# Graph attention on one core: the first three turned A^T pairs move into the set-up's last block

## The chip, the core and the metric

The kernel runs on 1 core of one Trainium2 chip. A core has five engines that run at the same time, each with its own queue of instructions: TensorE (PE, matrix products; its weight loads are shown as PEld), VectorE (DVE), ScalarE (ACT), GpSimd (POOL) and SyncE (SP). In this kernel POOL and SP mostly issue transfers (DMA) between the device's memory and the on-chip memory. An instruction waits until the work that it needs, on another engine or of a transfer, has been done; behind it the whole queue of its engine waits. [...]

The metric is the device time of one execution, in microseconds (us). The time before is 2067.35 us, the median of 3 runs (2067.16 to 2067.58).

## The reference

Two layers on N = 4096 nodes with 512 features; the change is in the first, a graph attention with H = 8 heads of 64 features. Cut to what matters:

```python
feats = jnp.einsum('nf,hfo->hno', X, W)
s_self = jnp.einsum('hno,ho->hn', feats, a_self)
s_neigh = jnp.einsum('hno,ho->hn', feats, a_neigh)
dense = s_self[:, :, None] + s_neigh[:, None, :]
dense = jnp.where(dense > 0, dense, ALPHA * dense)
dense = dense * A[None, :, :]
attn = jax.nn.softmax(dense, axis=-1)
out = jnp.einsum('hij,hjo->hio', attn, feats) + b[:, None, :]
out = jnp.transpose(out, (1, 0, 2)).reshape(N, H * FH)
return jax.nn.relu(out)
```

The result is added to x and normalized by row. The second layer (an attention inside groups of 128 nodes) follows; the change does not touch it. A, the 4096x4096 adjacency, holds zeros and ones.

## The kernel before

The exponential of a score is a product of a factor of the row and a factor of the column, and the choice between the two slopes is a maximum. So the kernel never forms a softmax over N x N scores: for a tile of 128 neighbours j and a chunk of 1024 nodes it computes Q = max(p, d_j) * A^T on VectorE (L1386), and a mark (which of the two was larger, L1391 and L1395), and lets TensorE sum Q, A^T and the marks against tables of the features.

**Set-up** (the block of pools at L586 and after) makes these tables. It works in 8 blocks k of 4 tiles of 128 nodes:

- turn_rows transposes the rows of x (L650), and ScalarE copies them out (L653).
- features (L722) multiplies a tile with the weights; VectorE adds the bias (L733). exponentials turns the two scores of a tile into its factors: two products on VectorE (L664), then three exponentials on ScalarE (e_all L670, pu_j L671, d_all L672).
- scaled_features makes the two tables of a tile: one scaled on VectorE (L766), one split into two float32r parts, by ScalarE (L775) and VectorE (L776). Each two tiles POOL writes them to memory (g_d and f_d, L789).
- rows_of_exponentials turns the factors of a block into rows (L695 on TensorE, the copy pu_row on ScalarE L699, the write pu_d on POOL L703). columns_of_exponentials turns these rows back into columns in another order (L708) and VectorE copies them to pu_all (L709).
- In the last block also the column sums of the features are made: the sums of x times the weights (L561), a copy to S_part on ScalarE (L820), and after all features four small products to columns (L568) and S_col on VectorE (L827).
- parts_of_exponentials splits factors into parts on VectorE (nb_all L676, e_b and rest L683 to L690).
- Three loads of adjacency, a_b, four tiles each in 8-bit floats, are issued by POOL in between (L581, after blocks 1, 3 and 5).

**Pass 0** follows. A pass handles two heads; there are four, each over 4 chunks c of 1024 nodes. Inside a chunk the 32 tiles j are taken in groups of 8 (in pass 0). For a group TensorE does, in this order: the products of A^T (accf, L1406: 32 matmuls), the products of Q (acc, L1426: 128), the sums of the marks (dens, L1440: 32) and counts (ae, L1350: 16).

In pass 0, A^T does not exist yet: `bring` makes it. For a pair of tiles TensorE turns a_b by 8 transposes of 128x128, two 8-bit values seen as one bf16 (L1130), into a PSUM bank given by `misc`, and ScalarE casts the bank to the two tiles `at` (L1134), which POOL also writes to at_d for the later passes (L1135). The first group's four pairs are brought right before its Q, and then in each group two pairs of the next group before the Q products and two after the counts:

```python
if at_step == 0:
    for j in cycle:
        bring(0, 0, j)
```

`misc` takes the PSUM banks of a list in turn. The list holds one bank in set-up, and from pass 0 on a second, that of the pool opened with the accumulator ae. `at` comes from 6 buffers of the pool atp, and from a second pool with 6 more, which lies where set-up's tiles were; `ring` counts turns to choose between them. Q has 6 + 2 buffers in the same manner.

**What sets the order.** TensorE's instructions stand in the order in which the program issues them (manual_schedule). For the other engines a scheduler orders instructions by its own estimates, with every dependency kept; keep_in_program_order pins single ones. A tile that lies over memory of a closed pool waits for all who used that memory, transfers too: the first `at` of the second pool waits for set-up's last writes.

Of the kernel before, what the change touches and what calls it, by code (L numbers as in the profile page):

```python
# [19 lines left out]
P = 128  # L20
# [375 lines left out]
F32R = mybir.dt.float32r  # L396
# [8 lines left out]
def adjacency_streamed_path(  # L405
# [29 lines left out]
    nc = tc.nc  # L435
# [6 lines left out]
    BIG = 2.0**70  # L442
    MORE = 6
    FP8 = mybir.dt.float8e4
    C = 1024
    CT = C // P
# [4 lines left out]
    scale = 1.0 / float(F) ** 0.5  # L451
# [13 lines left out]
    at_d = dram.tile([NCH, NT, P, C], F32, name="at_d")  # L465
# [21 lines left out]
    ident_b = const.tile([P, P], BF16, name="ident_b")  # L487
# [3 lines left out]
    d_all = const.tile([P, NT, H], F32, name="d_all")  # L491
# [3 lines left out]
    nb_all = const.tile([P, NT, H], F32, name="nb_all")  # L495
# [75 lines left out]

    ats = {}
    a_bs = {}
    pools = {}
    pools["adj"] = first_pass.enter_context(tc.tile_pool(name="adjp", bufs=3, side="right"))

    def load_adjacency(c, j):

        a_b = pools["adj"].tile([P, CT, 4 * P], FP8, name="a_b8")
        a_bs[c, j] = a_b  # L580
        return nc.gpsimd.dma_start(  # L581
            a_b, adj[ts(c, C), j * P : (j + 4) * P].rearrange("(t p) n -> p t n", p=P)
        )


    with tc.tile_pool(name="setup1", bufs=1, side="right") as one, tc.tile_pool(  # L586
        name="setup2", bufs=2, side="right"
# [69 lines left out]
        def exponentials(k, u, sc):  # L657

            j = 4 * k + u
            if u == 0:  # L660
                pu_js[k] = two.tile([P, 4, 2, H], F32, name="pu_j")
            st = small.tile([P, 5, H], F32, name="st")
            for lo, hi, w in ((0, 3, 1), (3, 5, 0)):
                nc.vector.tensor_tensor(  # L664
                    st[:, lo:hi].rearrange("p k (q h) -> p k q h", q=2),
                    sc[:, None, :, :, w].to_broadcast([P, hi - lo, 2, H // 2]),
                    powers[:, lo:hi].rearrange("p k (q h) -> p k q h", q=2),
                    OP.mult,
                )
            nc.scalar.activation(e_all[:, j], st[:, 0:2], AF.Exp)  # L670
            nc.scalar.activation(pu_js[k][:, u], st[:, 3:5], AF.Exp)  # L671
            nc.scalar.activation(d_all[:, j, :], st[:, 2], AF.Exp)  # L672
# [19 lines left out]
        def rows_of_exponentials(k):  # L692
            pr = pss.tile([2 * H, 4, P], F32, name="ps_set")
            for u in range(4):
                nc.tensor.transpose(  # L695
                    pr[:, u, :], pu_js[k][:, u].rearrange("p k h -> p (k h)"), ident
                )
            row = rows[k] = late.tile([2 * H, 4 * P], F32, name="pu_row")
            nc.scalar.copy(  # L699
                row.rearrange("p (q n k) -> p q k n", q=2, k=2),  # L700
                pr.rearrange("p (q k) n -> p q k n", q=2),
            )
            nc.gpsimd.dma_start(pu_d[:, ts(k, 4 * P)], row)  # L703

        def columns_of_exponentials(k):
            pc = pss.tile([P, 4, 2 * H], F32, name="ps_set")
            for u in range(4):
                nc.tensor.transpose(pc[:, u, :], rows[k][:, ts(u, P)], ident[: 2 * H, : 2 * H])  # L708
# [83 lines left out]
        for k in range(NB):  # L792
            for u in range(4):
                features(k, u)
                if u == (0 if k else 2) and k + 1 < NB:
                    turn_rows(k + 1)
                    if k + 2 < NB:
                        load_rows(k + 2)
                if u == 1 and k:
                    rows_of_exponentials(k - 1)  # L800
                if u == 2 and k:
                    columns_of_exponentials(k - 1)
                if u == 2 and k == 0:
# [309 lines left out]

    checked = []

    def bring(r, c, j):

        if r:
            at = ats[r, c, j] = ring("at", atp, 6).tile([P, C], F32R, name="at")
            nc.sync.dma_start(at.bitcast(F32), at_d[c, j])  # L1120
            return
        if j % 2:
            return
        if j % 4 == 0 and (c, j) not in a_bs:
            load_adjacency(c, j)
        pairs = a_bs[c, j - j % 4].rearrange("p t n -> p (t n)").bitcast(BF16)
        pairs = pairs.rearrange("p (t k n) -> p t k n", t=CT, k=2)[:, :, j % 4 // 2, :]
        pt = misc([P, CT, P], BF16)
        for t in range(CT):
            nc.tensor.transpose(pt[:, t, :], pairs[:, t, :], ident_b)  # L1130
        both = pt.rearrange("p t n -> p (t n)").bitcast(FP8).rearrange("p (n k) -> p n k", k=2)
        for k in range(2):
            at = ats[r, c, j + k] = ring("at", atp, 6).tile([P, C], F32R, name="at")
            nc.scalar.copy(at, both[:, :, k])  # L1134
            nc.gpsimd.dma_start(at_d[c, j + k], at.bitcast(F32))  # L1135

    def load_block():

        k = len(checked)
# [185 lines left out]
    def main_pass(r, ae=None, wide=4):  # L1325

        for c in range(NCH):
# [33 lines left out]
            for j0 in range(0, NT, wide):  # L1361
# [19 lines left out]
                for j in cycle:  # L1381
                    for h in range(2):
                        hh = 2 * r + h
                        q = qs[j, h] = ring("q", qp, 6).tile([P, C], F32, name="q")
                        d_j = d_all[:, j, hh : hh + 1]
                        nc.vector.scalar_tensor_tensor(  # L1386
                            q, p_row[h], d_j, ats[r, c, j].bitcast(F32), op0=OP.max, op1=OP.mult
                        )
                        mark = marks[j, h] = sgp.tile([P, C], FP8, name="mark")
                        if j % 4 == 3 and h == 1:  # L1390
                            nc.vector.tensor_scalar(  # L1391
                                mark, q, d_j, None, op0=OP.is_gt, saturate=False
                            )
                        else:
                            nc.scalar.activation(  # L1395
                                mark,
                                q,
                                AF.Sigmoid,
                                bias=nb_all[:, j, hh : hh + 1],
                                scale=BIG,  # L1400
                                saturate=False,
                            )
                for j in cycle:
                    for w in range(2):
                        for s in range(2):
# [142 lines left out]
```

## Time and profile before

| | before |
|---|---|
| median of 3 runs | 2067.35 us (2067.16 to 2067.58) |
| the profiled execution's own time | 2069.35 us |
| its span, from first to last instruction | 2067.6 us |
| TensorE busy | 2032.2 us (98%) |
| VectorE busy | 1670.1 us (81%) |
| ScalarE busy | 1540.2 us (74%) |
| mean granted TensorE clock | 0.993 |
| accf, 2048 matmuls | 494.4 us, 398 ns each |
| acc, 8192 matmuls | 902.8 us, 593 ns each |
| casts of A^T on ScalarE | 128, 120.1 us, 1025 ns each |
| end of the last features of set-up | 156.28 us |
| start of the first accf | 164.90 us |

All times in the profile are us from the start of the span unless marked ns. The chain that ended last is followed back from the last instruction: at each step to what released it, or to the instruction before it on its engine. "Issue" is time in which an engine waited for nothing that the profile shows. In rows of the timeline the bracket at the end tells how long the engine had been idle and what ended that. The granted clock is that of TensorE, as a share of full speed.

### The profile page before, as it was taken

The numbers are of one execution on the slowest core, as the hardware profiler recorded it, in microseconds if no ns is written. First come the engines' busy times: TensorE is split into PE (matmuls) and PEld (weight loads), VectorE is DVE, ScalarE is ACT, GpSimd is POOL, SyncE is SP. The second block draws the span as 40 slices with busy tenths as digits, with TensorE's granted clock in tenths as the row PEclk, the third lists the DMA queues.
The fourth block names the chain that finished last, engine by engine and source line by source line (L and its number), as shares of the span: only waits on it lengthen the run. The fifth ranks groups of instructions, "written<-read, shape, count | busy, mean of one in ns | idle before, by whom it ended". The sixth has DMA issues, their size and how long they took to land.

```text
span 2067.6 us, 38274 instructions
## 1 busy us (share of the span) xinstructions
PE 2032.2 (98%) x15086; PEld 1047.3 (51%) x15086; DVE 1670.1 (81%) x2125; ACT 1540.2 (74%) x1869; POOL 222.0 (11%) x361
## 2 busy tenths in 40 slices
PE   8999999999999999999999999999999999999997
PEld 6885555544445444444445444444454444445453
DVE  5667888888799998798999999999975984886654
ACT  3338888888878899788899899998885666567420
POOL 1223222222100000000000000000200210210111
PEclk9999999999999999999999999999999999999998
DMA  6989999999899999888999899989974773774211
GB/s 198 302 272 245 273 291 263 297 257 299 257 344 336 365 344 349 263 312 292 326 311 341 288 364 330 329 285 367 321 240 141 245 254 128 229 275 160 80 49 43
DMA packets 207371, 551.31 MB, mean 267 GB/s; under 512 B 24780, under 2 KB 65740, under 8 KB 207180
## 3 DMA queue, kind: packets, MB, share of 16 engines
q1 hardware_dynamic: 136716, 418.45, 57.8%
q0 software_dynamic: 62272, 121.91, 23.1%
q10 hardware_dynamic: 8192, 8.39, 1.2%
q8 instruction: 121, 1.98, 0.4%
q14 instruction: 70, 0.57, 0.1%
HBM read 491.79 MB, written 107.22 MB: 290 GB/s over the span
## 4 chain that ended last, share of the span: by engine, by line
PE 84%; DMA 6%; DVE 4%; issue 3%; ACT 2%; POOL 1%; ACTq 0%; POOLq 0%; DVEq 0%
PE acc L1426 36%; PE accf L1406 21%; PE ps_m L1067 5%; PE ps_fe L722 5%; PE ps_m L995 5%; PE dens L1440 5%; DMA at_d<-at 3%; DVE q L1386 3%; DMA a_b<-in_adj_dram 2%; PE ps_m L1022 1%; PE ps_m L1081 1%; PE ps_m L1130 1%; DMA xt_f<-in_x_dram 1%; PE ps_m L975 1%; PE ps_m L924 1%
## 5 line engine op out<-in xcount | busy, mean ns | idle before, releaser
L1386 DVE SCALAR_TENSOR_TENSOR q<-p_row,d_all,at 128x1024 f32<-128x1024 f32 x1024 | 1242.4, 1278 | 163.9 <-PE acc L1426 126.5
L1395 ACT ACTIVATE mark<-q,nb_all 128x1024 fp8e4<-128x1024 f32 x896 | 994.3, 1145 | 167.7 <-DVE q L1386 152.6
L1426 PE MATMUL acc<-q,g_s 128*32 128x512 f32 x8192 | 902.8, 593 | 1.1 <-DVE q L1386 0.4
L1426 PEld LDWEIGHTS acc<-q,g_s 128*32 128x32 f32 x8192 | 264.7, 110 | 593.8 <-issue 532.2
L1406 PE MATMUL accf<-at,f_s 128*128 128x512 f32 x2048 | 494.4, 398 | 1.9 <-issue 1.8
L1406 PEld LDWEIGHTS accf<-at,f_s 128*128 128x128 f32 x2048 | 380.2, 189 | 110.7 <-issue 29.1
L1151 ACT ACTIVATE ck<-ck,neg_half_f 128x1024 f32<-128x1024 f32 x128 | 145.9, 1140 | 27.1 <-DMA ck<-in_adj_dram 27.1
L1152 ACT ACTIVATE ck<-ck,neg_quarter 128x1024 f32<-128x1024 f32 x128 | 146.3, 1143 | 1.8
L1440 PE MATMUL dens<-mark,e_b 128*6 128x512 fp8e4 x2048 | 124.5, 379 | 1.6 <-ACT mark L1395 1.6
L722 PE MATMUL ps_fe<-w_sb_f,xT_f 128*128 128x264 f32 (+1 forms) x512 | 121.2, 395 | 4.5 <-ACT xT_f L653 4.5
L1134 ACT CAST at<-ps_m 128x1024 fp32r<-128x1024 fp8e4 x128 | 120.1, 1025 | 5.9 <-ACT mark L1395 3.1
L1067 PE MATMUL ps_m<-wvT,x1T 128*128 128x512 f32 x256 | 114.2, 594 | 0.0
L995 PE MATMUL ps_m<-x1T,M_sb 128*128 128x512 f32 x256 | 113.0, 595 | 0.9 <-ACT x1T L976 0.9
L722 PEld LDWEIGHTS ps_fe<-w_sb_f,xT_f 128*128 128x128 f32 x512 | 100.8, 200 | 18.8 <-ACT xT_f L653 4.9
L1271 POOL DMA_DIRECT2D hs_d<-hst x12 | 10.7, 893 | 832.3 <-DVE hst L1261 814.0
L1391 DVE TENSOR_SCALAR mark<-q,d_all 128x1024 fp8e4<-128x1024 f32 x128 | 95.8, 749 | 4.8
L1440 PEld LDWEIGHTS <-e_b 128*6 128x6 bf16 x2048 | 52.8, 86 | 81.8 <-issue 38.7
L1135 POOL DMA_DIRECT2D at_d<-at x128 | 69.0, 539 | 175.4 <-ACT at L1134 110.0
L995 PEld LDWEIGHTS ps_m<-x1T,M_sb 128*128 128x128 f32 x256 | 48.1, 190 | 62.5 <-issue 60.3
L1067 PEld LDWEIGHTS ps_m<-wvT,x1T 128*128 128x128 f32 x256 | 47.7, 190 | 57.1 <-issue 55.9
L1002 ACT ACTIVATE zT<-ps_m,zb 128x512 f32<-128x512 f32 x32 | 21.8, 682 | 71.1 <-PE ps_m L995 71.1
L1075 DVE TENSOR_TENSOR v_t<-ps_m,bv_row 128x512 f32<-128x512 f32 x32 | 21.9, 685 | 61.5 <-PE ps_m L1067 61.5
(185 smaller groups left out, 1084.2 us busy)
## 6 DMA issues: line engine op xcount, KB each, us to landing
at<-at_d SPq DMA_DIRECT2D x384, 512.0 KB, 6.1
f_s<-f_d SPq DMA_DIRECT2D x128, 512.0 KB, 7.4
at_d<-at POOLq DMA_DIRECT2D x128, 512.0 KB, 14.9
ck<-in_adj_dram SPq DMA_DIRECT2D x128, 512.0 KB, 5.4
g_s<-g_d SPq DMA_DIRECT2D x128, 256.0 KB, 5.9
f_d<-fst POOLq DMA_DIRECT2D x16, 1024.0 KB, 7.2
a_b<-in_adj_dram POOLq DMA_DIRECT2D x32, 512.0 KB, 16.1
p_row<-pu_d SPq DMA_DIRECT2D x32, 512.0 KB, 7.5
```

What stands on the lines that cost most here:

```text
L722: nc.tensor.matmul(pf[:, q, :, cols], tile_j(xTs[k][:, c].rearrange("p u n -> p (u n)"), u), w_sb[:, c, 4 * q : 4 * q + 4, cols], start=(c ...
L995: nc.tensor.matmul(pz, L1["M"][:, f, ts(c, P)], x1T[:, f, :], start=(f == 0), stop=(f == FC - 1),)
L1067: nc.tensor.matmul(pv, x1T[:, f, ts(u, P)], L1["wvT"][:, f, :], start=(f == 0), stop=(f == FC - 1),)
L1134: nc.scalar.copy(at, both[:, :, k])
L1151: tc.keep_in_program_order(nc.scalar.activation(ck, ck, AF.Square, bias=neg_half))
L1152: nc.scalar.activation(ck, ck, AF.Abs, bias=neg_quarter, accum_out=binp[:, k : k + 1])
L1386: nc.vector.scalar_tensor_tensor(q, p_row[h], d_j, ats[r, c, j].bitcast(F32), op0=OP.max, op1=OP.mult)
L1391: nc.vector.tensor_scalar(mark, q, d_j, None, op0=OP.is_gt, saturate=False)
L1395: nc.scalar.activation(mark, q, AF.Sigmoid, bias=nb_all[:, j, hh : hh + 1], scale=BIG, saturate=False,)
L1406: nc.tensor.matmul(accf[:, s, :], f_s[j // 4][:, j % 4, w, :], ats[r, c, j][:, ts(s, HB)], start=(j == 0 and w == 0), stop=(j == NT - 1 an ...
L1426: nc.tensor.matmul(acc[o : o + 32, s, :], g_s[j // 4][:, j % 4, h, o % FH : o % FH + 32], qs[j, h][:, ts(s, HB)], start=(j == 0), stop=(j ...
L1440: nc.tensor.matmul(dens[lo : lo + 6, :], e_b[:, j, 2 * r + h, :], marks[j, h][:, ts(s, HB)], start=(j == 0), stop=(j == NT - 1),)
```

## The change

`bring` moves ahead of set-up, and the first three of the four pairs of the first group are brought inside the last block of set-up: pair 1 after the second tile's features, pair 2 after the third's, pair 3 after the fourth's. Only the fourth pair is brought at the start of pass 0. The columns of the column sums come before rows_of_exponentials of the last block instead of after it. The first group's Q and marks are issued behind set-up's last scores on VectorE and last casts on ScalarE, by a hint to the scheduler (issue_after). `ring` counts turns from the beginning, so that the tiles of set-up count too.

In the scheduled program, the instructions of every engine are as many as before. On ScalarE the casts of the three pairs stand between set-up's last exponentials and copies, the copy of pu_row for the last block stands behind the last of them, and the marks of the first group, 14, follow the casts of the fourth pair in one row (before, the casts of the next pairs stood between them). On VectorE the first Q stands ahead of the last copy to pu_all. On POOL the writes of the three pairs stand between set-up's last writes: g_d and f_d of the last two tiles, then the two writes of pair 3, then pu_d of the last block.

```diff
     def ring(name, pool, n):
 
+        k = turns[name]
+        turns[name] += 1
         if name not in more:
             return pool
-        k = turns[name] % (n + more[name][1])
-        turns[name] += 1
-        return pool if k < n else more[name][0]
+        return pool if k % (n + more[name][1]) < n else more[name][0]
...
+    ends_of_setup = {}
...
+    def bring(r, c, j):
...
+        pt = misc([P, CT, P], BF16)
+        for t in range(CT):
+            nc.tensor.transpose(pt[:, t, :], pairs[:, t, :], ident_b)
+        both = pt.rearrange("p t n -> p (t n)").bitcast(FP8).rearrange("p (n k) -> p n k", k=2)
+        for k in range(2):
+            at = ats[r, c, j + k] = ring("at", atp, 6).tile([P, C], F32R, name="at")
+            ends_of_setup["ACT"] = nc.scalar.copy(at, both[:, :, k])
+            nc.gpsimd.dma_start(at_d[c, j + k], at.bitcast(F32))
...
-                nc.vector.tensor_tensor(
+                ends_of_setup["DVE"] = nc.vector.tensor_tensor(
                     st[:, lo:hi].rearrange("p k (q h) -> p k q h", q=2),
...
+                if k == NB - 1 and u:
+                    bring(0, 0, 2 * u - 2)
                 if k == NB - 1 and u == 1:
                     pS = pss.tile([P, H * FH], F32, name="ps_set")
...
-        rows_of_exponentials(NB - 1)
         pS = pss.tile([P, PR], F32, name="ps_set")
         sums_to_columns(pS, S_part)
         nc.vector.scalar_tensor_tensor(
             S_col, b_col, float(N), pS, op0=OP.mult, op1=OP.add
         )
+        rows_of_exponentials(NB - 1)
         columns_of_exponentials(NB - 1)
...
-    def bring(r, c, j):
...
                 if at_step == 0:
-                    for j in cycle:
-                        bring(0, 0, j)
+                    bring(0, 0, 6)
...
+                with ExitStack() as behind:
+                    if at_step == 0:
+                        for ins in ends_of_setup.values():
+                            behind.enter_context(tc.issue_after(ins.ins))
+                    for j in cycle:
...
```

The body of `bring` is the same but for the line that keeps the last cast; the loop over `cycle` that computes Q and marks is only indented.

More of the change, by code (lines that the diff above doesn't have):

```diff
@@ L583, in load_adjacency @@
         )
+    def bring(r, c, j):
+        if r:
+            at = ats[r, c, j] = ring("at", atp, 6).tile([P, C], F32R, name="at")
+            nc.sync.dma_start(at.bitcast(F32), at_d[c, j])
+            return
+        if j % 2:
+            return
+        if j % 4 == 0 and (c, j) not in a_bs:
+            load_adjacency(c, j)
+        pairs = a_bs[c, j - j % 4].rearrange("p t n -> p (t n)").bitcast(BF16)
+        pairs = pairs.rearrange("p (t k n) -> p t k n", t=CT, k=2)[:, :, j % 4 // 2, :]
+        pt = misc([P, CT, P], BF16)
[6 more added lines that the diff above has]
+            nc.gpsimd.dma_start(at_d[c, j + k], at.bitcast(F32))
     with tc.tile_pool(name="setup1", bufs=1, side="right") as one, tc.tile_pool(
@@ L1114, in adjacency_streamed_path @@
     checked = []
-    def bring(r, c, j):
[L1118 to L1135, printed above, removed]
     def load_block():
@@ L1380, in main_pass @@
                 qs = {}
[L1381 to L1392, printed above, removed]
-                            )
[L1394 to L1402, printed above, removed]
+                with ExitStack() as behind:
[3 more added lines that the diff above has]
+                    for j in cycle:
+                        for h in range(2):
+                            hh = 2 * r + h
+                            q = qs[j, h] = ring("q", qp, 6).tile([P, C], F32, name="q")
+                            d_j = d_all[:, j, hh : hh + 1]
+                            nc.vector.scalar_tensor_tensor(
+                                q, p_row[h], d_j, ats[r, c, j].bitcast(F32), op0=OP.max, op1=OP.mult
+                            )
+                            mark = marks[j, h] = sgp.tile([P, C], FP8, name="mark")
+                            if j % 4 == 3 and h == 1:
+                                nc.vector.tensor_scalar(
+                                    mark, q, d_j, None, op0=OP.is_gt, saturate=False
+                                )
+                            else:
+                                nc.scalar.activation(
+                                    mark,
+                                    q,
+                                    AF.Sigmoid,
+                                    bias=nb_all[:, j, hh : hh + 1],
+                                    scale=BIG,
+                                    saturate=False,
+                                )
```

## The prediction, on record before the changed kernel was run

> **What bounds the kernel now.** The page comes first: TensorE is busy for 98% of the span, and the chain that ended last lies mostly on it. Nothing that leaves TensorE's stream as long as it was can gain, and only a stretch in which TensorE waits, or runs slowly, has something to give.
>
> ```profile
> PE 2032.2 (98%) x15086; PEld 1047.3 (51%) x15086; DVE 1670.1 (81%) x2125; ACT 1540.2 (74%) x1869; POOL 222.0 (11%) x361
> PE 84%; DMA 6%; DVE 4%; issue 3%; ACT 2%; POOL 1%; ACTq 0%; POOLq 0%; DVEq 0%
> ```
>
> Next the chain in order of time, at the seam between set-up and pass 0, which the change touches (start, length, what).
>
> ```profile
> 152.52 3.78 PE ps_fe L722 x16
> ...
> 157.78 0.11 ACT pu_j L671
> 157.90 0.04 issue
> 157.94 0.28 PE ps_set L695
> 158.22 0.79 PE ps_set L568 x8
> 159.01 0.35 PE ps_set L708 x4
> 159.35 0.94 PE ps_m L1130 x8
> 160.29 0.02 issue
> 160.32 3.77 ACT at L1134 x4
> 164.09 0.04 issue
> 164.13 1.01 PE ps_m L1130 x8
> 165.14 9.54 PE accf L1406 x32
> ```
>
> The last features end at 156.28. TensorE then waits for ScalarE's exponentials (1.33 us) and twice for its casts of A^T (1.16 and 0.82): 3.3 us. Busy time in six stretches, cut where the granted clock changes, shows a second cost (columns: length, each engine, clock, DMA share, GB/s):
>
> ```profile
> 152.55:155.96 3.41, 3.41 (x16) 3.02 (x17) 1.95 (x6) 0.94 (x4) 0.00 (x0) 1.00 0.76 288
> 155.96:159.37 3.41, 2.08 (x20) 1.60 (x19) 2.87 (x11) 1.54 (x5) 0.22 (x1) 1.00 0.01 4
> 159.37:162.78 3.41, 2.25 (x21) 2.08 (x22) 2.83 (x13) 2.46 (x3) 2.63 (x5) 0.50 0.53 172
> 162.78:166.20 3.42, 2.60 (x16) 2.24 (x15) 3.42 (x5) 3.40 (x5) 1.90 (x4) 0.50 1.01 380
> 166.20:169.61 3.41, 3.41 (x9) 2.64 (x9) 3.41 (x4) 3.40 (x4) 0.58 (x2) 0.50 1.01 386
> 169.61:173.02 3.41, 3.41 (x16) 2.77 (x16) 1.64 (x2) 3.41 (x4) 1.92 (x3) 1.00 1.02 368
> ```
>
> The clock is 0.50 from 159.4 to 169.6, so the first 32 accf matmuls take 9.78 us; the second group's take 7.60, at clock 1.00. That is another 2.2 us. Last, ScalarE in order of time, because the change fills its queue:
>
> ```profile
> 160.32 5.59 ACT L1134 CAST at<-ps_m 128x1024 fp32r<-128x1024 fp8e4 x6 [1.46 <-PE ps_m L1130]
> 168.28 1.91 ACT L1134 CAST at<-ps_m 128x1024 fp32r<-128x1024 fp8e4 x2
> 188.20 1.91 ACT L1134 CAST at<-ps_m 128x1024 fp32r<-128x1024 fp8e4 x2
> 195.66 3.74 ACT L1134 CAST at<-ps_m 128x1024 fp32r<-128x1024 fp8e4 x4
> ```
>
> From 160.3 to 205 it idles only once, 2.44 us before 178.87. The second group's accf ends at 200.87, some 1.5 us after the cast of its last tile (195.66 + 3.74 = 199.40). So behind TensorE stands an engine almost as full.
>
> **The change, part by part.** No instruction is added; only places change.
>
> *TensorE.* The transposes of pairs 1 to 3 (L1130) go between the features of the last block. Eight cost 0.53 us at clock 1.00 (sixteen take 1.07 at 174.52). From the end of the features of the block's second tile (146.97): rows 0.44, pair 1 0.53, sums 0.99, features 3.77, columns 0.34, pair 2 0.53, features 3.78, pair 3 0.53: 157.9, and the column sums (0.79) 158.7. Each pair now uses one bank, as the second bank of the transposes does not exist yet in set-up; so pair 2 waits for the casts of pair 1, and so on. These are in time: on ScalarE, at 0.94 us each, pair 1's end at 150.9, pair 2's at 156.4 (one before the exponentials of a tile, one after), and TensorE wants the bank at 153.0 and 157.4.
>
> *ScalarE at the seam.* Pair 3's first cast runs 157.9 to 158.9, and the last exponentials, ready at about 158.3, queue behind it: 159.3. Then come fst (0.6), pair 3's second cast, 160.8, and only then the copy of pu_row (0.61): 161.4. The columns' transposes (0.35) need that copy: TensorE waits from 159.5 to 161.4. So the 1.33 us wait for exponentials is mostly gone (pair 3 and the sums cover it), the 1.16 and 0.82 are gone, and a new one of about 1.9 stands before the columns. Pair 4's transposes end at 162.4 (162.8 if the clock is low).
>
> *VectorE.* The first accf matmul waits for VectorE's copy of pu_all (L709), whose PSUM bank it takes over. In the new order the first Q (1.28 us) stands ahead of that copy. Features end 157.35; bias and scores 0.9, S_col 158.85, ae 0.48, L766 0.69, nb_all, L776 0.69, e_b 0.3: 161.1; Q 162.4; rest 0.31 and the copy 0.21: 162.9. So accf starts at about 163.0, not 164.90: 1.9 us gained.
>
> *Clock.* From 157.9 to 162.4 TensorE does little again. The row of 155.96 to 159.37 shows what that does: 2.08 us of small matmuls in 3.41 us, longest wait 1.33, and the clock fell. I take it to fall at the same place as the new wait, 162.8, and to rise when one stretch of 3.41 is full, 166.2: 1.6 us lost instead of 2.2. The ends are 0 (no fall) and 3.3 (one stretch more). accf would end at 163.0 + 7.6 + 1.6 = 172.2, against 174.68: 2.5 us gained so far, 4.1 without a fall.
> [...]
>
> *The gate.* Pair 4 is the first to write into the pool that lies over set-up's memory. Its first cast therefore waits for set-up's last writes to land, f_d and pu_d. Before, both were issued by 160.5, ahead of all writes of A^T; f_d landed 5.7 us after its issue, at 166.2, and the cast, due at 168.28, noticed nothing. Now POOL's queue has g_d, f_d, the two A^T writes of pair 3, and then pu_d. That L776 ends at 160.8 puts f_d's issue at 160.9 and its landing at 166.6. A write in this queue lands behind those before it: pu_d issued at 133.15 took 5.4 us and landed at 138.55, just after a_b (issued 126.75, 11.6 us: 138.35); with an empty queue it took 1.8. The A^T writes after f_d landed 1.3 to 2.1 us apart (167.5, 168.9, 170.2, 171.9). Two of them at 1.4 put pu_d at 169.4. The bounds are 166.6 (pu_d not held up) and 170.8 (2.1 each); I take 169.4, as the queue's own landings say it.
>
> *What stands behind the gate.* ScalarE's queue, in order: pair 4's casts (1.8), the table load (1.28), all 14 marks of group 0 (1.05 each, 14.7), four casts (3.7), four marks of group 1 (4.25), four casts (3.75). Before, the casts stood among the marks. From 169.4 that is: table 171.2, marks from 172.5, casts of pairs 4 and 5 done at 190.9 (before: 190.1), casts of group 1's last four at 198.9 (before: 199.4). accf of group 1 needs the last of them for its last four matmuls (0.95): it ends at 199.85 and not 200.87. Were ScalarE no limit, it would end 2.5 earlier, at 198.4. Of the 2.5 us that TensorE gains, 1.0 is left.
>
> *Hidden.* The three pairs' writes to at_d begin ten microseconds earlier, in a time when DMA moved little (0.01 share from 155.96); a_b's next two loads move ahead of pair 4's writes on POOL, and bv_row behind an f_s on SP. Their cover is the 25 us until group 1's transposes and accf read them (190): a_b, issued by 165, lands at worst 20.5 us later (its longest median in pass 0), at 185.5, against 12.4 at best; without that cover the lateness would fall on TensorE. The writes could also crowd f_d: they are done by 160, from the idle time. The turn counter picks the same pools. The bank of the transposes is the other one from pair 4 on; both are used in turn: 0 to 0.5 us.
>
> **Sum.** TensorE -1.9 (start) -0.6 (clock), ScalarE +1.5: -1.0 us, kept to the end, as what follows is TensorE back to back (its waits after 200 add up to some 8 us in 1867). The profiled execution took 2069.35 us, its span 2067.6; it is 2.0 above the median 2067.35. So 2068.35 for it, and 2066.35 for the median.
>
> **The rivals.** A: the gate opens early (166.6, pu_d not behind the A^T writes), and ScalarE is no limit: -2.5, and up to -4.1 with the clock kept; 2064.85, ends 2063.2 to 2065.5. For it: DMA stands idle from 156 and has less to do. Against: the landings above are in order. B, slower: the same gate later. accf of group 1 ends 30.4 us after it, so from 170.5 on each microsecond is one lost; at 172.0, with the two loads of a_b mixed in between, +1.5: 2068.85. For it: the latencies in this queue double to 15 us by 180. Against: those loads stand behind pu_d. C, no gain in the end: the waits of pass 0 at the boundaries of column blocks (0.7 us at 407, 1.1 at 510), which the chain follows back through DMA, keep their places: 2067.35.
>
> **How the numbers follow.** The likeliest 0.55 (2065.5 to 2067.2), A 0.22, B 0.15, C 0.08. The range for 8 in 10 takes in most of A and B: 2063.6 to 2068.9. What a measurement can tell from no change is about 0.2%, 4.1 us. Faster than 2063.2 needs A with the clock kept and one later wait gone: 0.08. Slower than 2071.5 needs the gate at 174.6: 0.05. Same: 0.87.
>
> **What would show it.** Right: TensorE waits about 1.9 us before the last columns and not before L695 and the second and third pair; ScalarE idles for some 8 us (161.4 to 169.4) ahead of pair 4's casts, released by a DMA; accf starts near 163.0 and ends near 172; accf of group 1 waits for casts. Wrong: casts of pair 4 before 167, or accf of group 1 without waits; a clock of 1.00 through the seam; or any wait in pass 0 that is over 1 us and was not there.

## The result: 0.16% slower, and a gate that opened later than its bounds

| | before | after |
|---|---|---|
| median, 22 runs each | 2068.58 us (2065.18 to 2071.67) | 2072.05 us (2068.93 to 2075.62) |
| ratio after / before | | 1.0016, 95% interval 1.0011 to 1.0022 |
| profiled execution: own time, span | 2069.35, 2067.6 us | 2069.89, 2068.1 us |
| mean granted clock | 0.993 | 0.997 |
| start, end of the first accf group | 164.90, 174.68 | 162.32, 176.36 |
| end of the second accf group | 200.87 | 202.70 |

By the ratio the changed kernel is slower by 3.3 us (0.16% of 2068.6; the medians lie 3.5 apart). That is within the 0.2% that the prediction took for the least that can be told from no change, but the interval leaves out 1, and the time is well above the forecast 2066.35. The two profiled executions are 0.5 us apart: the one of after lies near the bottom of its runs, the one of before above its median, so their ends can't be compared to a microsecond. The seam between set-up and pass 0 can.

The page of after, busy time and chain:

```profile
PE 2030.8 (98%) x15086; PEld 1045.0 (51%) x15086; DVE 1669.9 (81%) x2125; ACT 1539.7 (74%) x1869; POOL 223.2 (11%) x361
PE 90%; DVE 4%; DMA 2%; issue 2%; ACT 1%; POOL 0%; ACTq 0%; POOLq 0%; SPq 0%; DVEq 0%
```

TensorE is busy 1.4 us less than before (2032.2) in a span that is 0.5 longer: it waits more. The timeline of after at the seam, TensorE, ScalarE and POOL (in the bracket, the idle time before and what ended it):

```profile
157.05 0.61 PE L601 MATMUL ps_m<-ident_b,a_b 128*128 128x128 bf16 x8
...
160.99 0.41 PE L730 MATMUL ps_set<-ident_f,pu_row 16*128 16x16 f32 x4 [1.73 <-ACT pu_row L721]
161.34 0.62 PE L601 MATMUL ps_m<-ident_b,a_b 128*128 128x128 bf16 x8
162.32 7.33 PE L1412 MATMUL accf<-at,f_s 128*128 128x512 f32 x24 [0.37 <-DVE pu_all L731]
172.84 3.52 PE L1412 MATMUL accf<-at,f_s 128*128 128x512 f32 x8 [3.19 <-ACT at L605]
...
160.34 0.60 ACT L721 COPY pu_row<-ps_set 16x512 f32<-16x512 f32 x1
171.78 1.93 ACT L605 CAST at<-ps_m 128x1024 fp32r<-128x1024 fp8e4 x2 [10.84 <-DMA pu_d<-pu_row]
...
160.91 0.77 POOL L811 DMA_DIRECT2D f_d<-fst  x1
161.67 1.09 POOL L606 DMA_DIRECT2D at_d<-at  x2
162.75 0.51 POOL L725 DMA_DIRECT2D pu_d<-pu_row  x1
163.25 1.93 POOL L582 DMA_DIRECT2D a_b<-in_adj_dram  x2
```

The first row is pair 3's transposes, the row at 161.34 pair 4's. Read the view from the third group upwards. POOL issues pu_d at 162.75, behind pair 3's two writes; it lands 8.8 us later. ScalarE idles 10.84 us for that landing and casts pair 4 from 171.78. TensorE began accf 2.58 us earlier than before, but after 24 matmuls (six tiles) it stands 3.19 us, because the seventh tile is pair 4's. The clock makes it worse. Busy time in stretches of after (columns as before: length, PE, PEld, DVE, ACT, POOL, clock, DMA share, GB/s):

```profile
159.37:162.78 3.41, 1.42 (x14) 1.19 (x15) 3.31 (x12) 1.57 (x3) 2.62 (x5) 1.00 0.73 271
162.78:166.19 3.41, 3.41 (x10) 2.70 (x9) 3.41 (x8) 0.00 (x0) 2.41 (x3) 0.52 0.98 338
166.19:169.61 3.42, 3.42 (x15) 2.48 (x13) 3.42 (x4) 0.00 (x0) 0.00 (x0) 0.98 1.01 279
169.61:173.02 3.41, 0.22 (x2) 0.18 (x2) 2.21 (x2) 1.24 (x2) 0.00 (x0) 1.00 1.12 148
173.02:176.43 3.41, 3.41 (x11) 2.38 (x12) 0.00 (x0) 3.38 (x4) 1.11 (x2) 0.52 1.10 213
```

It falls once after the quiet stretch before accf (1.42 us busy in 3.41) and once more after the stand at the seventh tile (0.22 us busy in 3.41). The 32 matmuls take 7.33 + 3.52 = 10.85 us, 3.25 more than the 7.60 of a group at clock 1.00; before they took 9.78. So the first group ends at -2.58 (start) + 3.19 (wait) + 1.07 (clock, 10.85 - 9.78) = +1.68 us against before, the second at +1.83.

### The profile page after: what moved, and what is told of

Same layout as the page of the kernel before. It is cut to its first block, busy times and chain, and to the rows that moved or that the text cites. A ratio compares the mean times of both kernels' runs of the same rounds, so it can differ in the third digit from the quotient of the medians.

```text
span 2068.1 us, 38268 instructions
## 1 busy us (share of the span) xinstructions
PE 2030.8 (98%) x15086; PEld 1045.0 (51%) x15086; DVE 1669.9 (81%) x2125; ACT 1539.7 (74%) x1869; POOL 223.2 (11%) x361
## 4 chain that ended last, share of the span: by engine, by line
PE 90%; DVE 4%; DMA 2%; issue 2%; ACT 1%; POOL 0%; ACTq 0%; POOLq 0%; SPq 0%; DVEq 0%
PE acc L1432 40%; PE accf L1412 23%; PE ps_m L1091 5%; PE dens L1446 5%; PE ps_m L1019 5%; PE ps_fe L744 4%; DVE q L1392 2%; PE ps_m L1046 1%; PE ps_m L601 1%; PE ps_m L1105 1%; DMA xt_f<-in_x_dram 1%; PE ps_m L999 1%; PE ps_m L948 1%; PE ps_m L1263 1%; PE ae L1353 1%
```

## The experiments

**Theory G, the gate.** pu_d queued behind pair 3's writes holds the cast of pair 4, TensorE stands at the seventh tile, and the clock falls again. **Rival S:** ScalarE's queue, with 14 marks in a row and casts behind them, costs the time. **Rival N:** what is lost or won at the seam does not reach the end. And each part of the change may have its own share.

For all kernels the *seam* is the time from where the last features make way on TensorE (in the changed kernel the start of pair 3's transposes, 0.16 us before the last features' modelled end) to the end of the second accf group. That takes out what happens earlier. For the kernel before, 1.06 us (two pairs of transposes at 0.53, which the others do between the features) is taken off so that the same work is counted: 200.87 - 156.12 - 1.06 = 43.69. Where the third pair is not in set-up, the seam begins at the next instruction behind the last features. "Cast" is the start of pair 4's cast, counted from the same point; "wait" is TensorE's at the seventh tile.

| kernel | cast | wait | seam | against 43.7 | ratio to before, 95% |
|---|---|---|---|---|---|
| before | | 0 | 43.69 | | |
| before again | | 0 | 43.61 | -0.1 | 1.0001 (0.9992 to 1.0010) |
| after | 14.73 | 3.19 | 45.65 | +2.0 | 1.0016 (1.0011 to 1.0022) |
| after again | 14.66 | 2.36 | 45.56 | +1.9 | 1.0010 (1.0001 to 1.0019) |
| after, third time | 14.55 | 2.24 | 45.20 | +1.5 | one run |
| pu_d first | 10.74 | 0 | 40.62 | -3.1 | 0.9984 (0.9975 to 0.9993) |
| two pairs in set-up | 10.06 | 0 | 39.61 | -4.1 | 0.9981 (0.9972 to 0.9990) |
| two pairs, third between | 10.15 | 0 | 40.34 | -3.4 | 0.9979 (0.9970 to 0.9988) |
| loads later | 13.45 | 3.46 | 45.33 | +1.6 | 0.9998 (0.9990 to 1.0007) |
| load ahead of pu_d | 22.27 | 9.93 | 53.50 | +9.8 | 1.0047 (1.0032 to 1.0062) |
| casts between marks | 14.73 | 3.15 | 45.24 | +1.5 | 1.0006 (0.9997 to 1.0015) |
| rows before sums | 14.74 | 2.33 | 45.34 | +1.6 | 1.0012 (1.0003 to 1.0021) |
| no hint | 20.17 | 4.96 | 51.63 | +7.9 | 1.0047 (1.0033 to 1.0061) |

### The changed kernel again, and the kernel before again

> The changed kernel once more, with nothing edited, to see how far its seam repeats. Gate theory (the first cast of pair 4 waits until pu_d, queued on POOL behind pair 3's two writes, has landed; the products of A^T then stand still at the seventh tile, and the clock falls a second time): that cast begins at 171.8 us give or take 1, TensorE waits some 3 us for it, the first group of accf ends at 176.4 give or take 1.5, with the clock at 0.50 in two separate stretches; ratio to before 1.0011 to 1.0022. Rival, that the 3.2 us wait was an accident of one profile: the cast begins before 170 or the wait is under 1.5 us, and the ratio is still 1.0016, so that the loss lies elsewhere.

The cast begins at 173.00, 0.2 us past what was expected, because set-up ended 1.29 us later than in the first profile; counted from there the cast and the second group are within 0.1 us of it. The wait is 2.36 and the two clock losses are 3.14 together (8.08 + 2.66 - 7.60). The first group ends at 176.72. The ratio, 1.0010, is just under the expected range. G holds; the wait was no accident.

> The changed kernel a third time. Gate theory: the cast of pair 4 waits for pu_d until 14 to 15.5 us after the start of pair 3's transposes, and from there to the end of the second accf group it is 45.2 to 45.9 us (45.65 and 45.56 in the two profiles so far). If the loss varies with the clock: one fall less or more, 44.0 or 47.3. The start of the seam itself lies anywhere in 157.0 to 158.4, as set-up's first features ran at one or the other clock.

The cast is at 14.55 and the seam at 45.20, as expected of G. But here the clock fell once, for 6.8 us, and not again at the second half; the first group ended at 175.56, and then the *second* one waited for casts:

```profile
194.37 3.92 PE L1412 MATMUL accf<-at,f_s 128*128 128x512 f32 x16
199.02 4.00 PE L1412 MATMUL accf<-at,f_s 128*128 128x512 f32 x16 [0.74 <-ACT at L605]
```

So two paths leave the gate: the one over the seventh tile, and ScalarE's queue, whose last casts let the second group end 30.65 us after the cast of pair 4 (203.02 - 172.37). In the first profile of after the second group ended 30.92 us after the cast (202.70 - 171.78): there the direct path, with its second fall of the clock, is the longer by some 0.3 us, here ScalarE's is.

> The kernel before once more, nothing edited. The seam of the changed kernel, counted from the end of the last features to the end of the second accf group, is 1.9 us longer than in the one profile of before, while the times differ by 2 to 3.5 us. If that profile of before was typical: the stretch from the end of the last features (156.28) to the end of the second accf group (200.87) is again 44.6 us give or take 0.3, and TensorE waits again for marks at 401 (0.6) and 509 (1.0). If it was not (its own time was 0.8 above the median of before): the stretch is 43 to 44 us, or the two waits are gone, so that the end comes 1 to 2 us earlier. Ratio 0.9991 to 1.0009.

From the end of the last features (156.57) to the end of the second group (201.08) it is 44.51 us: the seam of before is typical. The waits for marks are not. At the end of the first column block this execution waits three times:

```profile
401.74 0.38 PE L1440 MATMUL dens<-mark,e_b 128*6 128x512 fp8e4 x1 [0.65 <-ACT mark L1395]
402.78 0.39 PE L1440 MATMUL dens<-mark,e_b 128*6 128x512 fp8e4 x3 [0.66 <-ACT mark L1395]
403.81 0.39 PE L1440 MATMUL dens<-mark,e_b 128*6 128x512 fp8e4 x4 [0.65 <-ACT mark L1395]
```

and its accf is 2.4 us later than in the first profile of before from there, while at the next block it takes 1.6 back. Such swings, one or two microseconds between executions of one program, are why ends of two profiles are not compared here.

### pu_d ahead of pair 3's writes

```diff
-            nc.gpsimd.dma_start(at_d[c, j + k], at.bitcast(F32))
+            write = partial(nc.gpsimd.dma_start, at_d[c, j + k], at.bitcast(F32))
+            if (c, j) == (0, 4):
+                held.append(write)
+            else:
+                write()
...
         rows_of_exponentials(NB - 1)
+        for write in held:
+            write()
         columns_of_exponentials(NB - 1)
```

> The changed kernel with one queue order undone: pair 3's two writes to at_d are issued behind pu_d instead of ahead of it. Gate theory: pu_d is issued about 1 us earlier and lands at 167 to 168.5, the cast of pair 4 begins there, the seventh tile is in time, and the first group of accf ends at 162.3 + 7.6 + 1.6 for one fall of the clock = 171.5 us; that is 4.8 below the changed kernel's 176.4 and 3.1 below before's 174.68. The end follows: 2066 to 2067.5 us, ratio to before 0.9980 to 0.9992. Rival S (the loss comes from ScalarE's queue, 14 marks in a row and casts behind them): the first group may end earlier, but the second group's accf waits for casts and ends within 1 us of the changed kernel's 202.7; ratio 1.001 to 1.002. Rival N (the seam does not reach the end, what is gained there is lost at the column blocks' ends): the second group ends near 198 and the ratio is still 1.000 to 1.002.

Timeline of this kernel (its own line numbers):

```profile
167.90 1.93 ACT L607 CAST at<-ps_m 128x1024 fp32r<-128x1024 fp8e4 x2 [6.84 <-DMA f_d<-fst]
...
162.44 9.20 PE L1420 MATMUL accf<-at,f_s 128*128 128x512 f32 x32 [0.36 <-DVE pu_all L737]
```

pu_d landed 5.7 us after its issue instead of 8.8, the cast waits for f_d, the 32 matmuls run in one piece, and the clock falls once, to 0.50 from 163.34 to 166.75. The first group ends at 171.64 (171.5 expected), the second at 197.78. Beside the changed kernel on the same chip the time is 2067.30 against 2072.64, 5.3 us less, for 4.9 us less at the seam; against the kernel before 0.9984. Rival N falls for a step of this size: it reached the end. This edit also moved some casts among the marks on ScalarE, so S is left to the next run but one.

### One more load ahead of pu_d

```diff
+        tc.keep_in_program_order(load_adjacency(0, 12))
         rows_of_exponentials(NB - 1)
```

> The changed kernel with one more transfer put ahead of pu_d on POOL: the load of a_b that followed it (tiles 12 to 15) is issued first. Nothing else changes its place on any engine. Gate theory: pu_d lands only after that load, whose landing took 16.4 us from its issue in the changed kernel: at about 163.8 + 16 = 180 us, bounds 175 (one microsecond per queue step) and 184; the cast of pair 4 begins there, and the first two groups of accf end later by as much as the cast begins later than 171.8, that is by some 8 us (3 to 12); the end rises by that less at most 3 for waits at the column blocks' ends. Rival S (ScalarE's queue of marks and casts behind the seam sets the loss): the same shift would come, but only in the second group, the first group's end staying at 176.4. Rival (pu_d is not what the cast waits for): no shift, 176.4 and 202.7.

```profile
180.54 1.93 ACT L605 CAST at<-ps_m 128x1024 fp32r<-128x1024 fp8e4 x2 [18.38 <-DMA pu_d<-pu_row]
...
181.60 3.78 PE L1413 MATMUL accf<-at,f_s 128*128 128x512 f32 x8 [9.93 <-ACT at L605]
```

With one load ahead of it, pu_d takes 15.4 us. The cast begins 8.76 us later than in after, the first group ends 9.02 later and the second 9.07 (set-up's later end makes 1.22 of each). One microsecond at the gate is one at both groups, already at the first. The time rises by 9.7 us (ratio 1.0047, three runs), for 9.8 at the seam. That is the gate in the other direction, and not S.

### ScalarE's order alone

```diff
-                if at_step == 0:
-                    bring(0, 0, 6)
...
                     for j in cycle:
+                        if at_step == 0 and j == 4:
+                            bring(0, 0, 6)
                         for h in range(2):
```

> The changed kernel with ScalarE's order alone edited: pair 4 is brought between the Q of tile 3 and of tile 4, so that seven marks run ahead of its casts, in the time in which ScalarE stood still, and six casts follow in a row. POOL's order stays, pu_d behind pair 3's writes. Gate theory: the cast of pair 4 still waits for pu_d, begins at 171.5 to 173, and the first group of accf ends at 176.0 to 177.5; the second group follows 26.3 us later; ratio to before 1.0008 to 1.0025. Rival S (ScalarE's queue is what costs): seven marks, 7.4 us, are taken off the queue behind the gate, and the second group of accf ends at 198 to 200; ratio 0.998 to 1.000.

Seven marks now run while ScalarE used to stand still:

```profile
166.15 6.09 ACT L1401 ACTIVATE mark<-q,nb_all 128x1024 fp8e4<-128x1024 f32 x5 [0.18 <-DVE q L1392]
172.15 1.91 ACT L605 CAST at<-ps_m 128x1024 fp32r<-128x1024 fp8e4 x2
...
173.19 3.19 PE L1412 MATMUL accf<-at,f_s 128*128 128x512 f32 x8 [3.15 <-ACT at L605]
```

The cast starts 0.2 us after pu_d's landing (163.12 + 8.8 = 171.9), right behind the marks. ScalarE is freed of 7.4 us behind the gate, and little moves: first group 176.38 (after: 176.36), second 202.66 (202.70). Set-up ended 0.37 us later here, so both are some 0.4 us sooner when counted from there, where S expected 3 to 5; 0.3 of that is a smaller clock loss (7.35 + 3.19 against 7.33 + 3.52). S falls as the cause; ScalarE's queue is a second limit close behind the first, and it starts from the same gate. The ratio, 1.0006 (0.9997 to 1.0015), is a little under the 1.0008 to 1.0025 that was expected of G; the two ranges overlap.

### The loads of a_b behind pair 4's writes

```diff
-            load_adjacency(c, j)
+            with ExitStack() as behind:
+                if (c, j) in ((0, 12), (0, 16)):
+                    behind.enter_context(tc.issue_after(pair_4[0].ins))
+                load_adjacency(c, j)
```

(pair_4 keeps the write of tile 7.)

> The changed kernel with the two loads of a_b that follow pu_d on POOL held behind pair 4's own writes; all other queues stay in the same order. It tells whether those loads slow the writes ahead of them. If they do (pu_d's 8.8 us hold about 2 us of mixing): pair 3's second write and pu_d land 1.3 to 2.1 us apart as the writes before them did, the cast of pair 4 begins at 169.4 to 170.3, the wait at the seventh tile is 0.7 to 1.6 us, and the first group of accf ends at 172.5 to 173.3, or 1.6 later if the clock falls again; ratio to before 0.999 to 1.0008. If they do not: cast at 171.8 and first group's end at 176.4, as in the changed kernel, ratio 1.0011 to 1.0022.

DMA issues of after, the issues at 162.2 and 162.75 us (median us to landing, last column; x2 holds both of pair 3's writes), and then of this kernel, at 163.2 and 163.7:

```profile
at_d<-at POOLq DMA_DIRECT2D x2, 512.0 KB, 8.0
pu_d<-pu_row POOLq DMA_DIRECT2D x1, 32.0 KB, 8.8
```

```profile
at_d<-at POOLq DMA_DIRECT2D x2, 512.0 KB, 7.4
pu_d<-pu_row POOLq DMA_DIRECT2D x1, 32.0 KB, 7.5
```

pu_d takes 7.5 us here, and 8.6 to 8.8 in the five profiles in which the loads follow it directly (after three times, casts between marks, rows before sums). So transfers queued *behind* a write slowed it by 1.1 to 1.3 us. That gate, 13.45, is still a little later than the 12.4 to 13.3 that was expected (169.4 to 170.3, from 157.05). The rest of the expectation was missed: the wait is 3.46 (0.7 to 1.6 expected) and the first group ends 18.29 us into the seam (15.4 to 17.9 expected, 19.31 in after). TensorE reached the seventh tile sooner and waited longer, and the clock, at 1.00 over the first 24 matmuls, fell 2.2 us into the wait:

```profile
163.28 5.78 PE L1418 MATMUL accf<-at,f_s 128*128 128x512 f32 x24 [0.37 <-DVE pu_all L737]
172.51 3.78 PE L1418 MATMUL accf<-at,f_s 128*128 128x512 f32 x8 [3.46 <-ACT at L609]
```

The seam is 0.3 us shorter than in after. The ratio, 0.9998, says 2.5 us less than the repeat of after on the same chip (1.0010); the intervals overlap, and whether the rest is real is open.

### The other two parts of the change, each undone

Rows of the exponentials before the column sums again:

```diff
+        rows_of_exponentials(NB - 1)
         pS = pss.tile([P, PR], F32, name="ps_set")
...
-        rows_of_exponentials(NB - 1)
         columns_of_exponentials(NB - 1)
```

> The changed kernel with its second part undone: the rows of the exponentials of the last block are again turned ahead of the column sums. The scheduler also puts the first Q further ahead on VectorE. Gate theory: the copy of pu_row still follows pair 3's second cast, pu_d still follows pair 3's writes; g_d and f_d are issued up to 1.3 us later, behind the Q, and everything behind them too: the cast of pair 4 at 172 to 174 (with the features' end as in the changed kernel), the first group's end at 176.4 to 178.5, ratio 1.001 to 1.003. Rival (the order of the column sums was a part of the loss): the columns' 1.7 us wait goes and the ratio is below 1.0005.

The gate stays at 14.74 (the profile puts the cast's wait down to a Q on VectorE that had long been done; pu_d landed at 172.5, 0.2 us before the cast) and the seam is 45.34. The 1.73 us wait ahead of the columns only split: 0.99 ahead of the last row and 0.94 ahead of the columns. g_d and f_d were not later as expected, so the first Q did not delay them. The first group ends at 175.89, sooner than expected, as the clock fell only once, and the second then waits 0.73 us for casts, as in the third profile of after. The order of the column sums has no measurable share.

Without the hint (issue_after) on the first Q and marks:

```diff
                 with ExitStack() as behind:
-                    if at_step == 0:
-                        for ins in ends_of_setup.values():
-                            behind.enter_context(tc.issue_after(ins.ins))
+                    if False:
+                        pass
                     for j in cycle:
```

> The changed kernel with its third part undone: without the hint, the scheduler puts four Q and one mark, with two table loads more, among set-up's last work, and one load of a_b ahead of set-up's last writes. Gate theory: one table load and mark more stand ahead of set-up's last exponentials (2 x 1.28 + 1.05 = 3.6 us on ScalarE), accf starts 2 to 4 us later than 162.3, and pu_d, behind the load of a_b, lands at 176 to 184; the first group ends at 180 to 188, ratio 1.003 to 1.007. Rival (the queue of 14 marks that the hint makes is what costs, so that to undo it gains): the second group of accf ends before 201, ratio below 1.0005.

As expected of G: ScalarE loads tables twice more ahead of set-up's last exponentials, accf starts at 165.89, pu_d, behind a load of a_b, gates the cast at 177.83, and the ratio is 1.0047. The hint is needed by the change, and was no cause of the loss.

### Only two pairs in set-up

```diff
-                if k == NB - 1 and u:
+                if k == NB - 1 and u in (1, 2):
                     bring(0, 0, 2 * u - 2)
...
                 if at_step == 0:
+                    bring(0, 0, 4)
                     bring(0, 0, 6)
```

> The changed kernel with only pairs 1 and 2 in set-up; pair 3 is brought with pair 4 at the start of pass 0. Pair 3's writes are then behind pu_d, and its casts behind the copy of pu_row. Gate theory: pu_d lands at 166.5 to 168, the columns no longer wait for a cast (the 1.7 us wait ahead of L730 goes), accf starts at 161.5 to 162.5 and its first group ends at 171 to 172, ratio to before 0.9978 to 0.9992. Rival S (ScalarE's queue): two casts more stand behind the seam, and the second group's accf ends no earlier than before's 200.9; ratio 1.000 to 1.002. Rival (three pairs inside the features are what gains): accf starts later than 163.5, as TensorE waits for pair 3's casts, and the ratio is 0.9995 to 1.001.

```profile
160.03 0.28 PE L717 MATMUL ps_set<-ident_f,pu_j 128*16 128x128 f32 x1 [0.52 <-ACT pu_j L693]
161.01 0.42 PE L730 MATMUL ps_set<-ident_f,pu_row 16*128 16x16 f32 x4 [0.70 <-ACT pu_row L721]
...
162.54 8.92 PE L1413 MATMUL accf<-at,f_s 128*128 128x512 f32 x32
```

The 1.73 us wait shrinks to 0.70 (0.52 stands ahead of the last row), pu_d is free of pair 3's writes, and the seam is the shortest, 39.61. Without the third pair in set-up the change gains 4.1 us at the seam, 0.9981 in the time (0.9972 to 0.9990). What the third pair cost was mostly the place of its two writes: with it in set-up and pu_d first, the seam is 40.62, only 1.0 us longer.

Pair 3 between the rows and the columns of the last block, instead of at the start of pass 0:

```diff
         rows_of_exponentials(NB - 1)
+        bring(0, 0, 4)
         columns_of_exponentials(NB - 1)
```

> The kernel with two pairs in set-up, and pair 3's transposes between the rows and the columns of the last block instead of behind the columns, to use TensorE's 0.7 us wait for the copy of pu_row. Gate theory: POOL's and ScalarE's orders are as with pair 3 behind the columns, pu_d is free of pair 3's writes; that wait shrinks to 0.2, accf starts 0.3 to 0.6 us earlier relative to the end of the last features, and the second accf group ends 39.0 to 39.4 us after the place of pair 3 in the changed kernel (39.6 with pair 3 behind the columns, 45.65 in the changed kernel), if the clock falls once as there. Ratio to before 0.9972 to 0.9988. Rival (VectorE's copy of pu_all or the gate at f_d is next to bind): the second group ends where it did, 39.6, and the ratio is that of two pairs in set-up, 0.9981 give or take 0.0009.

The columns' wait shrinks to 0.26 as meant, but a new one comes:

```profile
161.52 0.61 PE L601 MATMUL ps_m<-ident_b,a_b 128*128 128x128 bf16 x8 [1.37 <-ACT at L605]
```

Pair 4's transposes wait for pair 3's casts. By the code they share a bank: set-up's list has one, and the first call of misc in pass 0 gives it again. accf starts 5.0 us into the seam, later than the 4.3 of the version above and not sooner as expected. The seam is 40.34, not 39.2; the ratio, 0.9979, is that of the version above within its interval. The expectation's seam was missed; its ratio was met all the same, which shows that the ratio can't tell such versions apart.

Three versions beat both kernels, before and after: pu_d first, and the two with two pairs in set-up. At 0.9979 to 0.9984 their intervals overlap; by the seam the simplest, pair 3 left at the start of pass 0, is best.

## Why the prediction was wrong, point by point

*TensorE's start: right in kind.* A wait ahead of the columns was forecast at 1.9 us and measured at 1.73; accf was forecast at 163.0 and began at 162.32. The gain was 2.58, not 1.9.

*The gate: the step that failed.* The prediction named the right wait, the right transfer and the right queue: the cast of pair 4, pu_d, two writes ahead of it. Its size was wrong, and past its upper bound: 169.4 (166.6 to 170.8) against 171.78. f_d landed at 167.2, not 166.6; the first of pair 3's writes landed 1.4 us behind it and the second 2.7 behind the first, where the row gave 1.4 each; 0.5 us lie between that landing and the cast. That is 0.6 + 1.3 + 0.5 = 2.4 us. The 1.3 is the loads of a_b behind pu_d: with the loads later the second write landed 1.6 behind the first and pu_d took 1.1 to 1.3 us less. The prediction had set that aside ("those loads stand behind pu_d"); standing behind did not help. Why f_d took 6.3 us instead of 5.7 is not shown. Under *Hidden* the moved writes were to be done by 160; the last was issued at 156.67 and landed 4.9 us later, at 161.6.

*The path behind the gate: half right.* The prediction followed only ScalarE's queue (its term of +1.5 us), and had the second group end 30.4 us after the gate. Where that path decided, it measured 30.65 (after, third time). It left out the shorter path, from the cast straight to the seventh tile. With its own numbers nothing would have come of that: a tile is ready 1.06 us after its cast begins (172.84 - 171.78), so at 170.5, and TensorE would have come to it at 163.0 + 5.7 for 24 matmuls + 1.6 for the clock = 170.3. With the cast at 171.78 TensorE stands 3.19 us, and in two of the three profiles of after the stand costs the clock again.

*The clock: the second term mis-sized.* It was forecast as a gain of 0.6 (one fall, 1.6 lost instead of 2.2). Measured losses in the three profiles of after are 3.25, 3.14 and 2.62: the upper end, 3.3, was nearly reached, in the first two by a second fall behind the stand, in the third by one fall that lasted 6.8 us. The longest wait ahead of the first fall was 1.73 us. The prediction read the fall from a row of before (2.08 us of work in 3.41, longest wait 1.33). In all three profiles of after a fall came at this place too, but the row was not a sure guide: with the loads later, the same 1.73 us wait cost no clock. In them the first fall comes at 162.93, 161.79 and 161.38, and the clock then stays at 0.50 for 3.4, 6.8 and 6.8 us; what sets the moment and the length, no run shows.

*The sum.* Forecast -1.9 - 0.6 + 1.5 = -1.0; measured -2.58 (start) + 1.07 (clock) + 3.19 (TensorE's wait, in place of ScalarE's +1.5) = +1.68 at the first group, and +1.83 at the second. One of the prediction's own signs of being wrong came: a wait of over 1 us in pass 0 that was not there before. Of the 5.7 us between 2066.35 and 2072.05, 1.2 are the median of before, which stood at 2067.35 after three runs and at 2068.58 after 22.

*The rivals.* B is what came at the seam: the gate at 172.0, with the loads of a_b mixed in, and +1.5 us (measured 171.78 and +1.83; the loads made about half of the delay). It had 0.15, and its evidence against was the reading that failed. A's gate (pu_d not behind the writes) is what the first edit brought about, and it gave A's gain: 2.5 to 4.1 us forecast, 3.3 by the ratio. C's waits at the column blocks (0.60 us at 401 and 1.04 at 509 in the first profile of before) did not keep their places: they wait for marks, and in the three profiles of after there are none. So these blocks give the seam's loss back, by an amount that varies: of the +1.83 us, +1.06 are left at the accf behind the first block (404.60 against 403.54), and behind the second the changed kernel is 0.75 ahead (510.98 against 511.73).

*What stays open.* The seam is 1.5 to 2.0 us longer. The ratios say 3.3 us (2.3 to 4.6) in one session and 2.1 us (0.2 to 3.9) in the other. The five ratios of kernels with a seam 1.5 to 2.0 us longer go from 0.9998 to 1.0016, on average 1.0008 (1.7 us), so nothing beyond the seam is shown, and nothing rules out another microsecond. Nor do the profiles, as far as single executions can tell, show the loss arriving at the end: the spans of before are 2067.6 and 2068.7, those of after 2068.1, 2068.8 and 2068.4, and the first two of these executions of after are among the fastest of their series. That the seam counts in the time is shown by larger steps alone, pu_d first and the load ahead of it. Set-up itself may hold a part: its second row of features took 7.37 us in the first profile of before and in that of after, but 9.06 in the repeat of after (the last section) and 8.99 or 9.06 in seven of the eight edited kernels; whether that is chance, these profiles can't tell.

## What to carry to other kernels

When work is moved ahead of the last writes of a stage, look for who waits until those writes have *landed*: here a tile that lies over the stage's memory, for which ScalarE stood 10.84 us. Here the smallest write set the gate, as it came last in the queue: the 32 KB of pu_d took 8.8 us to land behind pair 3's two writes of 512 KB, and 5.7 ahead of them. The two loads of 512 KB right behind it moved it too, by 1.1 to 1.3 us. Then follow every path that leaves the gate, the short one first, and ask of each gap whether TensorE's clock falls behind it: behind the stands of 3.19 and 2.36 us at the seventh tile it fell to 0.50, behind the one of 2.24 it stayed at 1.00. Where you can, order the writes so that the one that somebody waits for goes first: here that was a gain of 4.9 us at the seam with the same work.

## What the runs showed of the hardware

The granted clock of one program at one place is not the same in every execution. In the three profiles of after it was 0.50 at the seam for 3.4 + 3.4 us, for 6.8 + 3.4 us and for 6.8 us; with the loads later it stayed at 1.00 until 171.2, inside the wait for the seventh tile. Such a difference appears already in set-up's first features, whose second row of 32 matmuls took 7.37 us in the first profile of after, at clock 1.00, and 9.06 in its repeat, 1.69 us more. At the seam one fall of 3.4 us cost 1.60 (pu_d first: 9.20 against 7.60), so by estimate this is one such fall:

```profile
31.70 7.37 PE L744 MATMUL ps_fe<-w_sb_f,xT_f 128*128 128x264 f32 x32
```

```profile
31.28 9.06 PE L744 MATMUL ps_fe<-w_sb_f,xT_f 128*128 128x264 f32 x32
```

From there to the end of set-up all work of the repeat lies 1.3 us later. A change of one or two microseconds is read from the length of its own stretch, not from where the stretch ends.
